# The turns of a quantized mixture of experts: down products ahead of the gate products, token copies behind rounding, more buffers

## The chip, the cores and the metric

The kernel runs on one core of a Trainium2 chip. The metric is the device time of one launch in microseconds, from the runs of the kernel; the profile comes from one further execution.

The engines go by their short names: PE is TensorE, which multiplies matrices; PEld is its loading of the stationary operand; DVE is VectorE; ACT is ScalarE; POOL is GpSimd; SP is SyncE, which only issues transfers. Each has its own list of instructions, and semaphores order them against each other.

## The reference, cut to what matters

The whole program is a decoder of two layers with six parts, over 2048 tokens (16 blocks of 128) of 256 numbers. The change touches the first part alone, a mixture of experts with weights of three values and activations of 8 bits:

```python
def activation_quant(x):
    scale = 127.0 / jnp.clip(jnp.max(jnp.abs(x), axis=-1, keepdims=True), 1e-05)
    return jnp.clip(jnp.round(x * scale), -128, 127) / scale
def weight_quant(w):
    scale = 1.0 / jnp.clip(jnp.mean(jnp.abs(w)), 1e-05)
    return jnp.clip(jnp.round(w * scale), -1, 1) / scale
def bitlinear(x, w):
    xn = rmsnorm(x, BIT_EPS)
    return activation_quant(xn) @ weight_quant(w).T      # in value
def bit_mlp(x, gate_proj_w, down_proj_w):
    gy = bitlinear(x, gate_proj_w)
    gate, y = jnp.split(gy, 2, axis=-1)
    return bitlinear(jax.nn.silu(gate) * y, down_proj_w)

shared_out = bit_mlp(x_flat, shared_gate_w, shared_down_w)
router_probs = softmax((rmsnorm(x_flat) * gate_norm_w) @ gate_w.T)
# two experts of eight per token, at most 320 tokens per expert, in the order of the tokens
for e in range(E):
    keep = sel & (jnp.cumsum(sel) <= capacity)
    routed += where(keep, w_e, 0.0)[:, None] * bit_mlp(x_flat, expert_gate_w[e], expert_down_w[e])
x = layernorm(x + routed + shared_out)
```

The gate projection makes 1024 numbers per token (512 for silu, 512 to multiply), the down projection goes from 512 back to 256.

## The kernel before

The part is the function `stage0`. Its instructions are issued in the order in which Python writes them (a manual schedule), so the code's order is each engine's order.

**Tiles, groups and turns.** A tile is 128 rows of tokens. There are 36 tiles in eight groups: three groups of the shared expert with four tiles (s0, s1, s2), four groups of routed tokens with five tiles for two experts (r0 to r3; the fifth tile is half one expert, half the other), and the last shared group s3. The main loop (L648) runs over turns: turn n works on tile n with its gate products, and on earlier tiles with the later steps.

For a tile the steps are these. `gated` (L481) multiplies the transposed tokens `xqT` with the expert's quantized weights, into the PSUM tiles ps_g and ps_y. `silu` (L492) is an ACTIVATE out of ps_g into "m_sg"; `hidden` (L497, the row L500) multiplies it on DVE with ps_y into "m_h"; `squares` (L502) sums the squares on ACT; `largest` (L506) takes the largest on DVE. When a group is through, POOL makes the reciprocal root (`K.rsqrt`) and `factors` (L510) the steps of the quantization. Then, six or seven turns after its gate products (`second`, L642), a tile is `rounded` (L517; on ACT for tiles 0 to 7, on DVE after that), `turn`ed (L524: four transposes on PE into ps_t), copied back one turn later by `turned` (L530, ACT, the row L532), multiplied by `down` (L534, PE into ps_o), and one turn after that `done` (L541) adds it to x, or scales it and stores it to `y_dram` for the routed tokens.

**Order within a turn, before.** In program order: the total of an expert's weights (`first_jobs`), the token transposes with their copies (`prepare` and `tokens`, L449), `rounded`, `done`, `squares`, `silu(n + 1)`, `hidden(n)`, `turn`, `turned`, `gated(n + 2)`, `down`, `largest`, the turn's jobs, `factors`. Read per engine this is:

- PE: total, token transposes (8 of them), turn, gate products, down, jobs;
- ACT: copy of the tokens (L455), rounded, done for odd routed tiles, squares, silu, turned, jobs;
- DVE: the factor of the tokens (L474), rounded, done, hidden, largest, jobs.

**Jobs.** Lists say which work beside the tiles goes into which turn. `made_in(e, n)` spreads the quantization of expert e's weights over turns n to n + 6: the sums of absolute values (`sum_down`, `sum_gate`), the `total` over partitions on PE, `means`, then `up` (ACT adds a large constant so that numbers are rounded, L232), `low` (DVE takes the constant off again and cuts at 1, L235) and `high` (DVE cuts at -1, L238). Experts begin in turns 0, 3, 5, 8, 10, 13, 15 and 18. Other jobs are the router (`logits`, `turn_logits`, and six pieces of `routes`, in turns 1 to 6), the quantization of the second half of the tokens (`quantized`), and `fetch`, which gathers a group's token rows from DRAM into "xe" by indirect transfers that POOL issues (L432), at the turn 6 for r0.

**Buffers.** The PSUM tags ps_g, ps_y, ps_t and ps_o have two buffers each. The tag "m_sg" has three, and it is used by `silu`, by `measured` and `quantized` (the quantization of the tokens, L250 and L269) and by `turn_logits`. The transposed tokens "xqT" have two.

Of the kernel before, what the change touches and what calls it, by code (L numbers as in the profile page):

```python
# [8 lines left out]
F32 = mybir.dt.float32  # L9
F16 = mybir.dt.float16  # L10
BF16 = mybir.dt.bfloat16
# [8 lines left out]
P = 128  # L20
NB = 16
D = 256
# [96 lines left out]
def stage0(K, ahead, late, late_dram):  # L119
# [6 lines left out]
    with ExitStack() as ctx:  # L126
# [70 lines left out]
        def weights(e):  # L197
            wf = raw[e].rearrange("p k n -> p (k n)")
            parts_of = (slice(0, 2 * 4 * D), slice(2 * 4 * D, 3 * 4 * D))
            n, bufs = ("", (5, 8)) if e < NE else ("_s", (1, 1))  # L200
            q = [K.new(wp, [P, k, 4 * D], BF16, t + n, bufs=m) for t, k, m in zip(("q", "q_d"), (2, 1), bufs)]
            qf = [t.rearrange("p k n -> p (k n)") for t in q]
            acc = K.new(small, [P, 2], F32, "w_acc")
            mean, s = (K.new(small, [P, 2], F32, t) for t in ("w_mean", "w_s"))
            back = K.new(small, [P, 2], F32, "w_back", bufs=10)
            made[e] = (q[0], q[1][:, 0, :].rearrange("p (k n) -> p k n", n=D), back)

            def sum_down():
                if e < 3:
                    nc.scalar.activation(qf[1], wf[:, parts_of[1]], AF.Abs, accum_out=acc[:, 1:2])  # L210
                else:
                    nc.vector.tensor_reduce(acc[:, 1:2], wf[:, parts_of[1]], AX.X, ALU.add, apply_absolute_value=True)

            def sum_gate():
                to = qf[0]
                if 3 <= e < NE:
                    to = K.new(work, [P, NB, P], BF16, "at_place", bufs=1).rearrange("p b n -> p (b n)")
                nc.scalar.activation(to, wf[:, parts_of[0]], AF.Abs, accum_out=acc[:, 0:1])

            def total():  # L220
                held[e] = K.new(ps, [P, 2], F32, "ps_o")
                nc.tensor.matmul(held[e], K.ones, acc, start=True, stop=True)

            def means():
                nc.vector.tensor_tensor(mean, held[e], parts, ALU.mult)
                nc.vector.tensor_scalar(mean, mean, 1e-5, None, ALU.max)
                nc.vector.reciprocal(s, mean)
                nc.vector.tensor_scalar(back, mean, 1.0 / 127.0, None, ALU.mult)

            def up(i):  # L230
                at = wf[:, parts_of[i]]
                nc.scalar.activation(at, at, AF.Identity, scale=s[:, i:i + 1], bias=magic)  # L232

            def low(i):
                nc.vector.tensor_scalar(qf[i], wf[:, parts_of[i]], MAGIC, 1.0, ALU.subtract, ALU.min)  # L235

            def high(i):
                nc.vector.tensor_scalar(qf[i], qf[i], -1.0, None, ALU.max)  # L238

            return SimpleNamespace(  # L240
                sum_down=sum_down, sum_gate=sum_gate, total=total, means=means, up=up, low=low, high=high,
            )
# [4 lines left out]
        )  # L247

        def measured(b):
            junk = K.new(work, [P, FF], F32, "m_sg", bufs=3)[:, :D]  # L250
            nc.scalar.activation(junk, x[b], AF.Square, accum_out=ss[:, b:b + 1])
            nc.vector.tensor_reduce(am[:, b:b + 1], x[b], AX.X, ALU.max, apply_absolute_value=True)

# [12 lines left out]
            nc.vector.tensor_copy(xq[:, four(g), D // 2:D // 2 + 1].bitcast(F32), ag.unsqueeze(2))  # L266

        def quantized(b):
            t = K.new(work, [P, FF], F32, "m_sg", bufs=3)[:, :D]  # L269
            nc.vector.tensor_scalar(t, x[b], rs_bit[:, b:b + 1], sc[:, b:b + 1], ALU.mult, ALU.mult)  # L270
            nc.vector.tensor_scalar(xq[:, b, :D // 2].bitcast(BF16), t, MAGIC, MAGIC, ALU.add, ALU.subtract)

# [17 lines left out]
                )  # L290

        def turn_logits():
            lgT = K.new(work, [P, FF], F32, "m_sg", bufs=3)
            nc.scalar.copy(lgT, held["lgT"])
            pt = K.new(ps, [P, 4, P], F32, "ps_t")
            for j in range(4):
                nc.tensor.transpose(pt[:, j, :], lgT[:, j * P:(j + 1) * P], K.ident)
            held["lg"] = pt.rearrange("p j (g e) -> p g j e", e=32)[:, :, :, :NE]
# [148 lines left out]
                g.backs.append(t)  # L447

        def tokens(g, t0):  # L449
            m = min(4, g.n - t0)  # L450
            pt = K.new(ps, [P, 8, P], BF16, "ps_t")
            for t in range(m):
                for k in range(KD):
                    nc.tensor.transpose(pt[:, 2 * t + k, :], g.rows[t0 + t][:, k * P:(k + 1) * P], K.identb)
            nc.scalar.copy(g.xqT[:, 2 * t0:2 * (t0 + m), :], pt[:, :2 * m, :])  # L455

        def prepare(g):

            if g.shared:
                g.use = [[(every, made[NE])]] * 4  # L460
                rows = [xq[:, 4 * g.i + t, :D // 2].bitcast(BF16) for t in range(4)]
                factor = a[:, four(g.i)]
                backs = [made[NE][2][:, i:i + 1].to_broadcast([P, 4]) for i in range(2)]
            else:
                w0, w1 = made[2 * g.i], made[2 * g.i + 1]
                g.use = [[(every, w0)]] * 2 + [[(every, w1)]] * 2 + [[(slice(0, 64), w0), (slice(64, P), w1)]]
                rows = [xe[g.i][:, t, :D // 2].bitcast(BF16) for t in range(5)]
                factor = xe[g.i][:, :, D // 2:D // 2 + 1].bitcast(F32).rearrange("p t c -> p (t c)")
                backs = g.backs
            g.bd = backs[1]  # L470
            g.xqT, g.rows = K.new(work, [P, 10, P], BF16, "xqT"), rows
            tokens(g, 0)
            g.s1 = K.new(small, [P, 5], F32, "m_s1")[:, :g.n]
            nc.vector.tensor_tensor(g.s1, factor, backs[0], ALU.mult)  # L474
            g.ss, g.am, g.rs, g.a2, g.s2, g.s3 = (
                K.new(small, [P, 5], F32, t)[:, :g.n] for t in ("m_ss", "m_am", "m_rs", "m_a2", "m_s2", "m_s3")
            )

        pg, py, sg, pt, hT, po = {}, {}, {}, {}, {}, {}

# [10 lines left out]

        def silu(n):  # L492
            g, t = tiles[n]
            sg[n] = K.new(work, [P, FF], F32, "m_sg", bufs=3)
            nc.scalar.activation(sg[n], pg[n], AF.Silu, scale=g.s1[:, t:t + 1])

        def hidden(n):  # L497
# [73 lines left out]
        w.means()  # L571
        w.up(0)
        prepare(groups[0])
        steps(1)
        for b in range(4, 8):
            quantized(b)
# [10 lines left out]
        w.low(1)  # L587
        load(2)
        w.high(1)
        for g in range(3):  # L590
            logits(g)


        jobs, first_jobs = {n: [] for n in range(N)}, {}
# [1 line left out]
        def job(n, f, *args):  # L596
            jobs[n].append((f, args))
# [21 lines left out]
            job(n + 6, call("high", 1))  # L619

        ws = {}
        job(0, logits, 3)
        job(0, turn_logits)
        for g in (2, 3):
            job(2 * g - 4, steps, g)
            for b in range(4):
                job(2 * g - 4 + b // 2, quantized, 4 * g + b)
        job(3, lambda: nc.sync.dma_start(xq_dram.rearrange("(b p) c -> p b c", p=P), xq))
        route = routes()
        for n in range(1, 7):  # L630
            job(n, next, route, None)
        for e, n in enumerate((0, 3, 5, 8, 10, 13, 15, 18)):
            made_in(e, n)
        job(11, ahead)
        job(6, fetch, 0, range(5))
        for g in groups[3:7]:
            job(g.start - 5, backs_of, g)
            if g.i:
# [6 lines left out]

        for n in range(max(second) + 3):  # L648
            r = second.get(n)
            if n in first_jobs:  # L650
                first_jobs[n]()
            if n + 2 in starts:
                prepare(starts[n + 2])
            if n + 1 in starts and starts[n + 1].n > 4:
                tokens(starts[n + 1], 4)
            if r is not None:
                rounded(r)
            if n - 2 in second:
                done(second[n - 2])
            if 0 < n <= N:  # L660
                squares(n - 1)
            if n - 1 in ends:
                g = ends[n - 1]
                K.rsqrt(small, g.rs, g.ss, 1.0 / FF, 1e-8, "m_rt")
            if n + 1 < N:
                silu(n + 1)
            if n < N:
                hidden(n)
            if r is not None:
                turn(r)  # L670
            if n - 1 in second:
                turned(second[n - 1])
            if n + 2 < N:
                gated(n + 2)
            if n - 1 in second:
                down(second[n - 1])
            if n < N:
                largest(n)
            for f, args in jobs.get(n, ()):
                f(*args)  # L680
            if n - 2 in ends:
                factors(ends[n - 2])


    def after_experts(work, small):
# [1573 lines left out]
```

## Time and profile before

| | us |
|---|---|
| runs of the kernel | 1493.09, 1498.34, 1503.92 (median 1498.34) |
| the profiled execution, its own time | 1500.89 |
| its span, first to last instruction | 1499.2 |
| mean granted TensorE clock in it | 0.933 |
| PE busy | 1285.9 |
| DVE busy | 817.3 |
| ACT busy | 662.9 |
| POOL busy | 441.3 |
| first gate product of tile 0 starts | 22.5 |
| last down product of the stage starts | 211.8 |

The span is cut into groups of equal instructions by line, engine and operation. "Busy" is the time in which an engine executes; waiting, branching and issuing transfers don't count. A wait is put down to what released it. The granted clock is the share of TensorE's full clock. Five of the six parts of the program, from about 212 us on, are not touched by the change.

### The profile page before, as it was taken

The numbers are of one execution on the slowest core, as the hardware profiler recorded it, in microseconds if no ns is written. First come the engines' busy times: TensorE is split into PE (matmuls) and PEld (weight loads), VectorE is DVE, ScalarE is ACT, GpSimd is POOL, SyncE is SP. The second block draws the span as 40 slices with busy tenths as digits, with TensorE's granted clock in tenths as the row PEclk, the third lists the DMA queues.
The fourth block names the chain that finished last, engine by engine and source line by source line (L and its number), as shares of the span: only waits on it lengthen the run. The fifth ranks groups of instructions, "written<-read, shape, count | busy, mean of one in ns | idle before, by whom it ended". The sixth has DMA issues, their size and how long they took to land.

```text
span 1499.2 us, 18888 instructions
## 1 busy us (share of the span) xinstructions
PE 1285.9 (86%) x6771; PEld 866.3 (58%) x6771; DVE 817.3 (55%) x1707; ACT 662.9 (44%) x1722; POOL 441.3 (29%) x531
## 2 busy tenths in 40 slices
PE   3366677889857999889999999999889999999995
PEld 1133344566633666566557777777677566665554
DVE  6868777989966677658444444446433411211114
ACT  5497674778933544332216554555543111111110
POOL 3223237667843645430232212122210200000003
PEclk9567898989988999998989999999999999999997
DMA  8164124111000000001000000001003123312102
GB/s 281 30 229 134 45 63 81 16 37 57 29 1 0 1 1 1 0 1 57 1 1 1 2 0 1 1 17 55 14 1 127 56 99 99 98 68 94 39 12 70
DMA packets 50541, 71.98 MB, mean 48 GB/s; under 512 B 10224, under 2 KB 39888, under 8 KB 50192
## 3 DMA queue, kind: packets, MB, share of 16 engines
q1 hardware_dynamic: 48272, 65.24, 13.1%
q0 software_dynamic: 2176, 5.55, 1.8%
q8 instruction: 53, 0.87, 0.2%
q14 instruction: 40, 0.33, 0.1%
HBM read 60.77 MB, written 5.80 MB: 44 GB/s over the span
## 4 chain that ended last, share of the span: by engine, by line
PE 66%; DVE 18%; ACT 5%; POOL 5%; issue 3%; DMA 1%; SPq 0%; ACTq 0%; DVEq 0%; POOLq 0%
PE ps_m L1648 7%; PE ps_y L2093 7%; PE ps_m L2082 7%; PE ps_g L2082 6%; PE ps_m L1668 4%; PE ps_m L1779 4%; PE ps_m L1236 2%; PE ps_s L1737 2%; PE ps_t L1770 2%; PE ps_y L1362 2%; PE ps_t L1759 2%; PE ps_seg L1304 2%; PE ps_y L1342 2%; DVE s L867 1%; PE ps_m L1330 1%
## 5 line engine op out<-in xcount | busy, mean ns | idle before, releaser
L2087 DVE TENSOR_TENSOR h<-h,ps_m 128x512 f32<-128x512 f32 x60 | 41.3, 689 | 226.5 <-PE ps_m L2082 226.5
L82 POOL TENSOR_SCALAR ln_t<-ln_mv 128x1 f32<-128x1 f32 (+1 forms) x84 | 16.2, 193 | 454.0 <-DVE ln_mv L90 309.5
L1750 ACT ACTIVATE s<-s,m 128x128 f32<-128x128 f32 x256 | 99.5, 391 | 53.7 <-DVE m L1744 53.7
L2086 ACT ACTIVATE h<-ps_g 128x512 f32<-128x512 f32 x60 | 35.8, 597 | 171.6 <-PE ps_g L2082 171.6
L2082 PE MATMUL ps_g<-xin,w 128*128 128x512 f32 x224 | 106.3, 592 | 0.0
L1754 POOL TENSOR_TENSOR s<-s,t 128x1024 f32<-128x1024 f32 x32 | 60.9, 1902 | 152.6 <-DVE t L1753 152.6
L2082 PE MATMUL ps_m<-xin,w 128*128 128x512 f32 x224 | 105.3, 592 | 0.0
L2093 PE MATMUL ps_y<-w,h 128*128 128x256 f32 x448 | 97.8, 379 | 0.0
L2093 PEld LDWEIGHTS ps_y<-w,h 128*128 128x128 f32 x448 | 85.1, 190 | 14.6 <-issue 3.3
L879 ACT ACTIVATE s<-s,m 128x128 f32<-128x128 f32 x256 | 83.2, 394 | 15.7 <-DVE m L874 15.7
L2082 PEld LDWEIGHTS ps_m<-xin,w 128*128 128x128 f32 x224 | 42.5, 190 | 51.4 <-issue 50.2
L2082 PEld LDWEIGHTS ps_g<-xin,w 128*128 128x128 f32 x224 | 42.0, 190 | 46.4 <-issue 45.0
L1740 DVE TENSOR_TENSOR s<-ps_s,hide 128x1024 f32<-128x1024 f32 x32 | 39.2, 1224 | 52.1 <-PE ps_s L1737 52.0
L1648 PE MATMUL ps_m<-ctxT,l1x_W_k 128*128 128x256 f32 x256 | 63.9, 398 | 1.6 <-DVE qT L1653 1.0
L1762 DVE COPY s<-ps_t 128x512 f32<-128x512 f32 x32 | 22.1, 690 | 76.4 <-PE ps_t L1759 76.4
L1648 PE MATMUL ps_m<-xT,half 128*128 128x256 f32 x256 | 61.2, 393 | 2.6 <-DVE qT L1653 1.9
L1668 PE MATMUL ps_m<-l1x_W_v,ctxT 128*128 128x512 f32 x128 | 62.1, 614 | 0.0
L1779 PE MATMUL ps_m<-half,oT 128*128 128x256 f32 x256 | 59.3, 385 | 0.0
L528 PE MATMUL ps_t<-ident,m_h 128*128 128x128 f32 x144 | 29.0, 336 | 34.5 <-ACT m_h L520 14.1
L1242 DVE SCALAR_TENSOR_TENSOR acc<-ps_m,l1a_conv_w,acc 128x508 f32<-128x508 f32 (+2 forms) x72 | 52.6, 735 | 10.6 <-ACT acc L1238 10.5
L2094 ACT COPY y<-ps_y 128x256 f32<-128x256 f32 x30 | 11.2, 372 | 104.7 <-PE ps_y L2093 66.2
L1648 PEld LDWEIGHTS ps_m<-xT,half 128*128 128x128 f32 x256 | 48.5, 194 | 11.2 <-DVE qT L1653 2.3
(497 smaller groups left out, 3116.9 us busy)
## 6 DMA issues: line engine op xcount, KB each, us to landing
w<-in_w_gate_dram SPq DMA_DIRECT2D x9, 1024.0 KB
w<-in_l1f_gateT_dram SPq DMA_DIRECT2D x14, 512.0 KB
w<-in_l1f_upT_dram SPq DMA_DIRECT2D x14, 512.0 KB
w<-in_l1f_downT_dram SPq DMA_DIRECT2D x14, 512.0 KB
w<-in_w_down_dram SPq DMA_DIRECT2D x9, 512.0 KB
ring<-y SPq DMA_DIRECT2D x128, 32.0 KB
y_dram<-y SPq DMA_DIRECT2D x20, 128.0 KB
x<-in_x_dram SPq DMA_DIRECT2D x16, 128.0 KB
```

The source lines that it names most:

```text
L879: nc.scalar.activation(at, at, AF.Exp, bias=m[h][:, i:i + 1])
L1242: nc.vector.scalar_tensor_tensor(accv[:, :, j:], pcv[:, :, :P - j], w.conv[:, c, TAPS - 1 - j:TAPS - j], accv[:, :, j:], ALU.mult, ALU.add,)
L1648: nc.tensor.matmul(pq[:, j, :], wt[k][:, at], src[:, k, :], start=(k == 0), stop=(k == KD - 1))
L1668: nc.tensor.matmul(pv, self.ctxT[:, k, b * P:(b + 1) * P], self.w.v[:, k, 512 * j:512 * j + 512], start=(k == 0), stop=(k == KD - 1),)
L1740: nc.vector.tensor_tensor(half(b, j), pss.rearrange("p r c k -> p (r c) k"), hide.unsqueeze(1).to_broadcast([P, 8, P]), ALU.add,)
L1750: nc.scalar.activation(at, at, AF.Exp, bias=m[j][:, i:i + 1], accum_out=t[j][:, i:i + 1])
L1754: nc.gpsimd.tensor_tensor(half(b, j), half(b, j), t[j].unsqueeze(2).to_broadcast([P, 8, P]), ALU.mult)
L1779: nc.tensor.matmul(py[b], oT[b][:, c, :], w.o[c // 4][:, c % 4, :], start=(c == 0), stop=(c == NC - 1))
L2082: nc.tensor.matmul(ps[:, j, :], m[k][:, c * P:(c + 1) * P], self.r.xin[:, k, e, cols], start=(k == 0), stop=(k == KD - 1),)
L2086: nc.scalar.activation(h, pg, AF.Silu)
L2087: nc.vector.tensor_tensor(h, h, pu, ALU.mult)
L2093: nc.tensor.matmul(pd, rows(c), w.down[c // 4][:, c % 4, :], start=(c == 0), stop=(c == FI // P - 1))
```

## The change

It has five pieces.

1. The order within a turn becomes: total, `rounded`, `turned`, copy of the tokens, `hidden`, `silu`, `turn`, `down`, `gated`, `squares`, `done`, `largest`, jobs, `factors`, `scaled`, then `prepare` and the token transposes. Per engine: PE has total, turn, down, gate products, jobs, token transposes; ACT has rounded, turned, copy of the tokens, silu, squares, done, jobs; DVE has rounded, hidden, done, largest, jobs, factor of the tokens.
2. `tokens` returns its copy as a function, which is called in the next turn. The transposes of a group start at the end of the third turn ahead of it, instead of the head of the second.
3. For experts 0 and 1 the low step is done by ACT (constant taken off), and the cut at 1 joins the cut at -1 on DVE.
4. `measured` and `quantized` get buffers of their own ("m_q", three of half the size), and "m_sg" gets four.
5. The logits move into turns 0 and 1, `turn_logits` to turn 1, the six pieces of `routes` to turns 2 to 7, and r0's `fetch` to turn 7.

```diff
             def low(i):
-                nc.vector.tensor_scalar(qf[i], wf[:, parts_of[i]], MAGIC, 1.0, ALU.subtract, ALU.min)
+                if e < 2:
+                    nc.scalar.activation(qf[i], wf[:, parts_of[i]], AF.Identity, bias=unmagic)
+                else:
+                    nc.vector.tensor_scalar(qf[i], wf[:, parts_of[i]], MAGIC, 1.0, ALU.subtract, ALU.min)
             def high(i):
-                nc.vector.tensor_scalar(qf[i], qf[i], -1.0, None, ALU.max)
+                if e < 2:
+                    nc.vector.tensor_scalar(qf[i], qf[i], 1.0, -1.0, ALU.min, ALU.max)
+                else:
+                    nc.vector.tensor_scalar(qf[i], qf[i], -1.0, None, ALU.max)
...
-            junk = K.new(work, [P, FF], F32, "m_sg", bufs=3)[:, :D]
+            junk = K.new(work, [P, D], F32, "m_q", bufs=3)
...
-            t = K.new(work, [P, FF], F32, "m_sg", bufs=3)[:, :D]
+            t = K.new(work, [P, D], F32, "m_q", bufs=3)
...
-            nc.scalar.copy(g.xqT[:, 2 * t0:2 * (t0 + m), :], pt[:, :2 * m, :])
+            return lambda: nc.scalar.copy(g.xqT[:, 2 * t0:2 * (t0 + m), :], pt[:, :2 * m, :])
...
-            sg[n] = K.new(work, [P, FF], F32, "m_sg", bufs=3)
+            sg[n] = K.new(work, [P, FF], F32, "m_sg", bufs=4)
...
-        for g in range(3):
-            logits(g)
-        job(0, logits, 3)
-        job(0, turn_logits)
+        for g in range(4):
+            job(g // 2, logits, g)
+        job(1, turn_logits)
-        for n in range(1, 7):
+        for n in range(2, 8):
             job(n, next, route, None)
-        job(6, fetch, 0, range(5))
+        job(7, fetch, 0, range(5))
...
         for n in range(max(second) + 3):
             r = second.get(n)
             if n in first_jobs:
                 first_jobs[n]()
-            if n + 2 in starts:
-                prepare(starts[n + 2])
-            if n + 1 in starts and starts[n + 1].n > 4:
-                tokens(starts[n + 1], 4)
             if r is not None:
                 rounded(r)
-            if n - 2 in second:
-                done(second[n - 2])
+            if n - 1 in second:
+                turned(second[n - 1])
+            if turned_tokens is not None:
+                turned_tokens()
+                turned_tokens = None
+            if n < N:
+                hidden(n)
+            if n + 1 < N:
+                silu(n + 1)
+            if r is not None:
+                turn(r)
+            if n - 1 in second:
+                down(second[n - 1])
+            if n + 2 < N:
+                gated(n + 2)
             if 0 < n <= N:
                 squares(n - 1)
...
-            if n + 1 < N:
-                silu(n + 1)
-            if n < N:
-                hidden(n)
-            if r is not None:
-                turn(r)
-            if n - 1 in second:
-                turned(second[n - 1])
-            if n + 2 < N:
-                gated(n + 2)
-            if n - 1 in second:
-                down(second[n - 1])
+            if n - 2 in second:
+                done(second[n - 2])
...
+            if n + 2 in starts:
+                scaled(starts[n + 2])
+            if n + 3 in starts:
+                prepare(starts[n + 3])
+                turned_tokens = tokens(starts[n + 3], 0)
+            if n + 2 in starts and starts[n + 2].n > 4:
+                turned_tokens = tokens(starts[n + 2], 4)
```

`scaled` is the product of the tokens' factors (L474 before), taken out of `prepare`.

More of the change, by code (lines that the diff above doesn't have):

```diff
@@ L292, in turn_logits @@
         def turn_logits():
-            lgT = K.new(work, [P, FF], F32, "m_sg", bufs=3)
+            lgT = K.new(work, [P, FF], F32, "m_sg", bufs=4)
             nc.scalar.copy(lgT, held["lgT"])
@@ L470, in prepare, with scaled @@
             g.bd = backs[1]
[L471 to L476, printed above, removed]
-            )
+            g.xqT, g.rows, g.first = K.new(work, [P, 10, P], BF16, "xqT"), rows, (factor, backs[0])
+            g.s1, g.ss, g.am, g.rs, g.a2, g.s2, g.s3 = (
+                K.new(small, [P, 5], F32, t)[:, :g.n] for t in ("m_s1", "m_ss", "m_am", "m_rs", "m_a2", "m_s2", "m_s3")
+            )
+        def scaled(g):
+            nc.vector.tensor_tensor(g.s1, *g.first, ALU.mult)
         pg, py, sg, pt, hT, po = {}, {}, {}, {}, {}, {}
@@ L573, in stage0 @@
         prepare(groups[0])
+        tokens(groups[0], 0)()
+        scaled(groups[0])
         steps(1)
@@ L627, in stage0 @@
                 job(2 * g - 4 + b // 2, quantized, 4 * g + b)
+        job(1, turn_logits)
         job(3, lambda: nc.sync.dma_start(xq_dram.rearrange("(b p) c -> p b c", p=P), xq))
-        route = routes()
-        for n in range(1, 7):
-            job(n, next, route, None)
         for e, n in enumerate((0, 3, 5, 8, 10, 13, 15, 18)):
             made_in(e, n)
+        route = routes()
+        for n in range(2, 8):
+            job(n, next, route, None)
         job(11, ahead)
-        job(6, fetch, 0, range(5))
+        job(7, fetch, 0, range(5))
         for g in groups[3:7]:
@@ L651, in stage0 @@
                 first_jobs[n]()
[L652 to L655 removed]
             if r is not None:
                 rounded(r)
[L658 to L659 removed]
+            if n - 1 in second:
+                turned(second[n - 1])
+            if turned_tokens is not None:
+                turned_tokens()
+                turned_tokens = None
+            if n < N:
[8 more added lines that the diff above has]
+                gated(n + 2)
             if 0 < n <= N:
```

## The prediction

> **What bounds the kernel now.** I read the page's 40 slices first: the change touches only the first stage (the quantized experts), so I looked for that stage's end and its busy shares. The last down product of the stage starts at 211.8 us; everything behind it (86% of the span) keeps its instructions, so a gain here counts once, in full. Then I cut the stage at the starts of the products L500 of tiles 0, 7, 22 and 35 (25.6, 80.5, 155.3, 200.3 us) and asked for the busy time per stretch. Columns: stretch, length, then PE, PEld, DVE, ACT, POOL, and the granted clock.
>
> ```profile
> 25.60:80.50 54.90, 21.98 (x109) 9.88 (x108) 40.79 (x122) 28.03 (x41) 10.38 (x8) 0.59 0.31 107
> 80.50:155.30 74.80, 47.80 (x222) 27.11 (x222) 56.27 (x124) 62.18 (x96) 23.92 (x45) 0.75 0.50 164
> 155.30:200.30 45.00, 30.71 (x193) 18.31 (x194) 31.57 (x70) 31.57 (x66) 11.01 (x19) 0.88 0.14 46
> 200.30:212.40 12.10, 9.78 (x71) 6.84 (x69) 7.71 (x21) 6.62 (x12) 1.33 (x2) 0.88 0.19 66
> ```
>
> No engine is full. DVE leads in the first stretch (14.1 us idle), ACT in the second (12.6 idle), nobody in the third (13.4 idle on both). So I read the view of waits of each stretch for the engine that leads it.
>
> First stretch, DVE (and ACT behind it):
>
> ```profile
> DVE m_sg L270 <- PE ps_t L297: 4.4, 1, 4.4
> DVE m_sg L270 <- ACT m_sg L504: 3.2, 1, 3.2
> DVE whose L411 <- PE ps_o L406: 2.8, 1, 2.8
> ACT m_h L520 <- DVE m_s L514: 7.7, 1, 7.7
> PE ps_y L487 <- DVE m_h L500: 14.2, 4, 5.8
> ```
>
> Two waits, 7.6 us, are for a free "m_sg" buffer: L270 shares its three with silu, `measured` and `turn_logits`. The last two lines show ACT and PE waiting for DVE.
>
> Second stretch:
>
> ```profile
> ACT xqT L455 <- PE ps_t L454: 12.6, 6, 3.4
> DVE x L546 <- PE ps_o L539: 11.8, 5, 3.2
> PE ps_t L528 <- ACT xqT L455: 2.7, 3, 1.1
> DVE m_s L474 <- DMA xe<-xq_dram,token: 2.6, 1, 2.6
> ```
>
> The first line is all of ACT's idle time: the copy of the transposed tokens stands at the head of ACT's turn, and PE reaches the transposes only after its own previous turn and the weight total. The second is DVE's: `done` stands ahead of `hidden`, and its down product is PE's last act of the turn before.
>
> Third stretch, waits and then the chain that ended last (start, us, what):
>
> ```profile
> DVE y L552 <- PE ps_o L539: 9.9, 7, 2.3
> ACT xqT L455 <- PE ps_t L454: 8.1, 3, 3.9
> ACT y L550 <- PE ps_o L539: 5.4, 5, 1.2
> DVE m_s L474 <- DMA xe<-xq_dram,token: 2.8, 1, 2.8
> ```
>
> ```profile
> 193.22 0.69 ACT m_hT L532
> ...
> 193.96 0.62 PE ps_o L539 x4
> ...
> 194.60 0.48 DVE y L552
> 195.09 0.67 DVE m_h L500
> ...
> 195.80 0.59 PE ps_y L487 x2
> 196.39 0.45 PE ps_o L539 x4
> ...
> 196.87 0.47 ACT y L550
> ```
>
> This is a ring through four engines: turned, down, done, hidden, gate products, down, done, squares, silu, turned. It closes at 198.53, 5.3 us for two turns.
>
> **What the Trainium skill says.** "TensorE: Matmul & The Clock Gate", section on the array of 32×32 sub-arrays: PE may pull weight loads ahead, but matmuls keep their order, and ACT and DVE take instructions strictly in order. The trace agrees: squares, silu and turned all sit behind the copy that waits 12.6 us. "Perfetto Trace Analysis", section Optimization Strategy under Identifying Performance Opportunities: equal bubbles that return can mean too few buffers; the two m_sg waits are that. The first page's section "What's actually happening" has PE at half clock until it has been busy for some microseconds; here the clock is 0.59 and 0.75 in stretches where PE is 40% and 64% busy, and the four transposes L528 take 1.11 us slow and 0.66 us fast. "SBUF — State Buffer", section "SBUF: two separate sides": DVE and POOL exclude each other on a shared port pair. L235 of expert 0 took 1.75 and 1.21 us while POOL worked on L395 (68.67 to 72.96), 1.22 and 0.69 otherwise.
>
> **The change, part by part.**
>
> *m_q beside m_sg (three buffers of its own, m_sg four).* The 4.4 and 3.2 us waits go: -7.6 on DVE, which leads there.
>
> *Low steps of experts 0 and 1 on ACT.* Two ACTIVATEs per expert. No row has this form; bounds are the row L232 (2.09 and 1.24 us, two pointer operands) above and L218 and L210 (1.90 and 1.05) below. I take 2.0 and 1.1, which is also the estimate from "ScalarE: Activation LUTs", section What ACT_TABLE_LOAD costs (280 ns + 0.833 per element with a pointer bias: 1.99 and 1.13). ACT +3.1 per expert. DVE loses 1.75 + 1.21 = 3.0 for expert 0, 1.9 for expert 1; `high` gains an operand and stays one pass (0.68 + 0.42). Expert 0's falls in turn 5, where ACT waits for DVE (28.0 busy of 54.9): hidden, -3.0. Expert 1's falls in turn 8, where ACT leads: +3.1. Behind it on ACT stand turn 9's rounding, turned and silu; PE waits for them.
>
> *Logits, turn_logits and routes a turn later; fetch in turn 7.* The moved work is equal: 16 matmuls, one copy (0.59), the DVE rows of the router, exp with its table loads, five gathers on POOL and the semaphores they wait for. The last piece (`whose`, `token`, 0.6 us, and the 2.8 us wait ahead of it) leaves the stretch before tile 7: -3.4 for that stretch, most of which the next one may pay as idle DVE time, where DVE has 18 us to spare. The gathers have less slack: issue to landing was 79.9 to about 88 us, and the transposes that need them stand two to three turns later, at some 5 us each. At nothing, up to +3. On SP the xq_dram store keeps turn 3; the weight load behind expert 0's and 1's low now waits for ACT instead of DVE, earlier in time.
>
> *Copies a turn later than their transposes.* In PE's order the eight transposes only move from the head of a turn to the end of the one before; what they pass is the weight total, which waits for ACT's last job. On ACT the copy moves behind rounded and turned. Eleven copies. In the second stretch six waits cost 12.6. The one at 123.57 (2.8) is partly the gather's landing (DVE L474 waits for the same DMA) and stays; of the other 9.8 I keep 1.7, since there are only two ps_t buffers and PE's turn transposes now wait for ACT's turned (0.7) after a token turn: -8.1.
>
> *Turned and down in front of the gate products, hidden in front of done, silu in front of squares.* Nothing is added. The ring above is cut: done no longer stands before hidden, so the 11.8 us (DVE, second stretch: not the leader, no gain of its own) and the 9.9 + 5.4 us (third stretch) lose their reason. The new wait: gate products now queue behind down, which waits for turned on ACT; silu of the next turn waits for them. From turned: 0.62 down + 0.55 first gate half (fast clock), while ACT has silu 0.57 and squares 0.62 to do. Even; so no stall at full clock.
>
> **Sum.** First stretch: -7.6 - 3.0 - 3.4 = -14.0; DVE then works 37 of 41 us, and I give 4 us back for waits that the trace doesn't show yet (means for the weight total, the cumulative sum's matmul): -10. Second: -8.1 + 3.1 = -5; at best -9.5 (all 12.6 gone, +3.1), at worst +3. Third: 13 turns at 3.46 us; the work of a turn at full clock is PE 0.66 + 0.62 + 1.1 = 2.4, DVE 31.57/13 = 2.4, ACT 2.4. I take 2.9, which leaves room for r3's gathers, whose 2.8 us wait stays: 13 x 2.9 = 38, -7 (between -2 and -11). Last: the drain has the same steps, 0. Together -22 us on the profiled execution's 1500.89 us (span 1499.2), which is 2.55 above the median of the runs, 1498.34: 1478.9 by its own scale, about 1477 by the median.
>
> **The rivals.**
>
> *A. The leading engine sets the pace, and only the buffers help.* I summed each turn's work on ACT and on DVE and took the larger: 172 us over turns 0 to 34, where the trace has 174.7 (25.6 to 200.3). By that count turns are already paced by their fullest engine, and reordering inside a turn gains little. For it: this agreement, and the second stretch, where ACT is 83% busy. Against: the third stretch, 45.0 against 40.4. It would give -9 us: 1489.
>
> *B. Full decoupling.* All engines run a turn ahead; each stretch comes to its leader's work plus 3 us: 41, 68, 36 instead of 54.9, 74.8, 45.0: about -30 to -36, 1464. Against: gathers and the long jobs (2 us ACTIVATEs) come in lumps.
>
> *C. Slower: the gate products behind down.* PE stays near half clock after 80 us. Then a turn on PE is 1.1 + 0.85 + 1.7, tokens and totals 0.4, and 0.5 waiting for turned with nothing else allowed past: 4.6 us. Over 28 turns (7 to 34) that is 129 us against 119.8: +9, and with only 3 us won in the first stretch +6: 1504. It decides once the granted clock is below about 0.6 in the second and third stretch; it was 0.75 and 0.88. For it: before, gate products never had to wait for the same turn's turned.
>
> *D. The change does nothing*, because a buffer ties the copy and the turn transposes together (two ps_t): within 3 us. I count it with A.
>
> **How the numbers follow.** Main case 0.5 (own range 1467 to 1488), A and D 0.24, B 0.19, C 0.07. Measured differences under about 1% (1483.4 to 1513.3) can't be told from no change. Faster by over 1%: 0.43 of the main case, B, and a little of A, 0.65. Slower by over 1%: 0.03, the tail of C. The rest, 0.32, is within. The range runs from B's 1461 to 1494, which leaves out C, part of D and B's best.
>
> **What would show it.** In the trace after: tile 7's product near 70 us instead of 80.5, no DVE wait for m_q; copies of tokens without more than 1 us of ACT idle before them, save r1 and r3; DVE not waiting for the down product; the third stretch under 40 us; the last down product near 190 us, and the rest unmoved at 1287 us. I am wrong if silu waits for gate products turn after turn (C), if ACT is over 90% busy in the second stretch at the same length (A), or if the gathers of r0 come late.

## The result and the profile after

The changed kernel takes 1481.08 us (median of 5 runs, 1476.46 to 1485.84), the kernel before 1498.34. The ratio is 0.9885, with an interval of 0.9847 to 0.9924; a second series gave 0.9891 (0.9871 to 0.9912). It is faster by 1.1%; 1477 us was predicted. But one of the three stretches of the stage became longer where the prediction had it shorter, and that stretch is what the experiments are about.

Stretches are read as before, at the starts of the product that makes the hidden values (now L507) of tiles 0, 7, 22 and 35, and at the end of the last down product (now L546). Busy time by stretch of the kernel after, columns as before (length; PE, PEld, DVE, ACT, POOL; granted clock):

```profile
23.90:68.60 44.70, 23.01 (x108) 10.68 (x107) 38.89 (x118) 32.22 (x45) 9.22 (x6) 0.71 0.42 143
68.60:146.20 77.60, 46.54 (x225) 27.68 (x225) 53.88 (x125) 62.63 (x92) 29.23 (x47) 0.69 0.48 158
146.20:184.30 38.10, 27.75 (x193) 16.81 (x190) 30.27 (x68) 31.28 (x66) 11.60 (x19) 0.96 0.16 51
184.30:195.80 11.50, 8.90 (x72) 6.55 (x72) 7.97 (x22) 7.50 (x15) 1.41 (x2) 1.00 0.23 82
```

First stretch 54.9 to 44.7, second 74.8 to 77.6, third 45.0 to 38.1, drain 12.1 to 11.5. In the second stretch ACT, its fullest engine, is busy for 62.6 us as for 62.2 before, and PE and DVE for less than before, so its 2.8 us are new idle time of these engines.

First stretch, the waits that answer to those of before (engine, line, releaser: us in total, times, longest):

```profile
PE ps_y L494 <- DVE m_h L507: 6.7, 3, 4.7
ACT m_h L527 <- DVE m_s L521: 6.1, 1, 6.1
DVE whose L415 <- PE ps_o L412: 1.9, 1, 1.9
```

The two waits of L270 for an "m_sg" buffer are gone. Second stretch:

```profile
POOL m_rt L82 <- ACT m_sg L511: 30.9, 2, 16.7
ACT xqT L462 <- PE ps_t L461: 12.0, 5, 7.1
DVE w_mean L225 <- PE ps_o L222: 11.3, 3, 6.5
...
DVE m_a L518 <- POOL m_rs L83: 9.0, 1, 9.0
PE ps_t L461 <- DMA xe<-xq_dram,token: 8.5, 5, 3.6
...
POOL m_b L452 <- DMA xe<-xq_dram,token: 4.6, 1, 4.6
```

DVE hardly waits for the down product here any more (0.5 us in place of 11.8), as forecast. But ACT's copy of the tokens still waits 12.0 us (12.6 before), and what stands behind that wait is new: PE waits 8.5 us at the token transposes for gathered rows, and DVE waits 9.0 us once for a root on POOL.

The timelines of DVE and POOL show that one wait (start, duration, engine, line; the idle time before it and its releaser in brackets):

```profile
76.66 0.43 DVE L242 TENSOR_SCALAR q_d<-q_d 128x1024 bf16<-128x1024 bf16 x1
86.09 0.16 DVE L518 TENSOR_TENSOR m_a<-m_am,m_rs 128x4 f32<-128x4 f32 x1 [9.01 <-POOL m_rs L83]
```

```profile
83.73 0.18 POOL L452 COPY m_b<-w_back 64x1 f32<-64x1 f32 x1 [4.65 <-DMA xe<-xq_dram,token]
...
84.74 0.19 POOL L82 TENSOR_SCALAR m_rt<-m_ss 128x4 f32<-128x4 f32 x1
85.02 1.04 POOL L83 TENSOR_TENSOR m_rs<-m_rt,mhalf 128x4 f32<-128x4 f32 x1
```

POOL had issued r0's five gathers (71.9 to 78.7 us), then stood in the copy of r0's weight scales L452 until they had landed, with the root of group s1 behind it. The copy reads only scales, no gathered rows, and yet the profile puts the end of its wait to the gathers; why it waits for them is not shown.

The timelines of POOL and PE around r1's gathers:

```profile
100.26 0.20 POOL L82 TENSOR_SCALAR m_rt<-m_ss 128x4 f32<-128x4 f32 x1 [14.20 <-ACT m_sg L511]
...
104.70 1.07 POOL L438 DMA_INDIRECT xe<-xq_dram,token  x1 [0.28 <-POOL m_b L452]
...
110.27 2.52 POOL L438 DMA_INDIRECT xe<-xq_dram,token  x1 [0.30 <-issue]
```

```profile
110.91 0.77 PE L461 MATMUL ps_t<-identb,xe 128*128 128x128 bf16 x4 [2.93 <-issue]
113.74 0.40 PE L461 MATMUL ps_t<-identb,xe 128*128 128x128 bf16 x2 [2.06 <-DMA xe<-xq_dram,token]
117.76 0.40 PE L461 MATMUL ps_t<-identb,xe 128*128 128x128 bf16 x2 [3.62 <-DMA xe<-xq_dram,token]
117.94 0.53 PE L222 MATMUL ps_o<-w_acc,ones 128*128 128x2 f32 x2
```

The gathers queue on POOL behind a root (L82) that waited 14.2 us for ACT's squares of tile 11. PE meets the rows before they are there and stands in order; the weight total L222 behind it is what DVE's 6.5 us wait for.

Third stretch, waits and the chain of work that ended last (start, us, what):

```profile
ACT xqT L462 <- issue: 5.4, 1, 5.4
...
PE ps_o L546 <- ACT m_hT L539: 4.1, 5, 2.0
DVE m_s L484 <- DMA xe<-xq_dram,token: 4.0, 1, 4.0
PE ps_t L461 <- DMA xe<-xq_dram,token: 3.8, 4, 1.1
```

```profile
174.00 1.02 ACT xqT L462
...
175.60 0.61 ACT m_sg L511 x2
176.21 0.58 ACT m_hT L539
176.79 0.58 ACT m_sg L502
177.37 0.57 ACT m_sg L511 x2
```

In this piece the chain is ACT's own work but for a pair of gate products at 175.07; `done` is not in it, and the ring through four engines is cut. Further on (179.8 to 184.4) it runs through POOL's root and DVE's factors. The wait of down for turned (4.1 us in five) is the new wait that the prediction named, small as it said. What is left is again gathers, those of r3; the 5.4 us at ACT's copy, for which the view names no releaser, stand before r3's copy too.

The profiled execution spans 1474.7 us, 24.5 less than before: 16.6 in the stage and 7.9 in the rest, whose instructions did not change. By the medians of the runs the gain is 17.3 us, near the stage's 16.6; the last section comes back to the rest.

### The profile page after: what moved, and what is told of

Read it like the earlier page. It is cut to its first block, busy times and chain, and to the rows that moved or that the text cites. A ratio compares the mean times of both kernels' runs of the same rounds, so it can differ in the third digit from the quotient of the medians.

```text
span 1474.7 us, 18916 instructions
## 1 busy us (share of the span) xinstructions
PE 1273.7 (86%) x6771; PEld 862.8 (59%) x6771; DVE 809.4 (55%) x1703; ACT 667.3 (45%) x1726; POOL 445.0 (30%) x531
## 4 chain that ended last, share of the span: by engine, by line
PE 64%; DVE 19%; POOL 6%; ACT 4%; issue 4%; DMA 2%; SPq 0%; DVEq 0%; POOLq 0%; ACTq 0%
PE ps_y L2108 7%; PE ps_m L2097 7%; PE ps_g L2097 7%; PE ps_m L1663 6%; PE ps_m L1794 4%; PE ps_m L1683 3%; PE ps_m L1251 3%; PE ps_s L1752 2%; PE ps_t L1785 2%; PE ps_y L1377 2%; PE ps_t L1774 2%; PE ps_y L1357 2%; PE ps_seg L1319 1%; DVE s L882 1%; PE ps_m L1345 1%
## 5 line engine op out<-in xcount | busy, mean ns | idle before, releaser
L82 POOL TENSOR_SCALAR ln_t<-ln_mv 128x1 f32<-128x1 f32 (+1 forms) x84 | 16.1, 192 | 451.6 <-DVE ln_mv L90 309.5
L2109 ACT COPY y<-ps_y 128x256 f32<-128x256 f32 x30 | 11.2, 372 | 104.7 <-PE ps_y L2108 64.6
L1663 PEld LDWEIGHTS ps_m<-ctxT,l1x_W_k 128*128 128x128 f32 x256 | 47.8, 195 | 9.3 <-DVE qT L1668 1.4
```

The lines of the kernel that those rows point to most:

```text
L1663: nc.tensor.matmul(pq[:, j, :], wt[k][:, at], src[:, k, :], start=(k == 0), stop=(k == KD - 1))
```

## The experiments

Theory P: time was lost because POOL stands in r0's scale copies until the gathers land. Theory G: the gathers of r1 to r3 come too late for transposes that now stand earlier. Rival Q: ACT is the bound of the second stretch, and waits elsewhere cost nothing. Each kernel was timed against the kernel before on the same chip. Stretches are of one profiled execution each; two executions of the changed kernel differ by up to 1.1 us in a stretch.

| kernel | first | second | third | whole, ratio to before (interval) |
|---|---|---|---|---|
| before | 54.9 | 74.8 | 45.0 | 1 |
| changed | 44.7 | 77.6 | 38.1 | 0.9885 (0.9847 to 0.9924) |
| changed, second series | 45.8 | 77.4 | 38.8 | 0.9891 (0.9871 to 0.9912) |
| scale copies of r0 first | 45.9 | 71.5 | 38.0 | 0.9880 (0.9855 to 0.9904) |
| gathers a turn earlier | 45.6 | 74.3 | 32.3 | 0.9832 (0.9806 to 0.9858) |
| both | 45.5 | 67.8 | 31.6 | 0.9805 (0.9781 to 0.9828) |
| low steps on DVE | 47.8 | 75.3 | 39.0 | 0.9922 (0.9905 to 0.9939) |
| both, copies at once | 45.3 | 67.8 | 34.8 | 0.9827 (0.9809 to 0.9845) |
| both, low of expert 1 on DVE | 45.7 | 68.5 | 32.5 | 0.9815 (0.9795 to 0.9834) |
| gathers ahead of the root | 45.9 | 68.7 | 33.5 | 0.9813 (0.9798 to 0.9829) |
| both, routes as before | 46.8 | 70.3 | 31.4 | 0.9812 (0.9796 to 0.9828) |
| before + buffers | 49.3 | 73.9 | 44.1 | 0.9954 (0.9936 to 0.9971) |
| before + order | 57.0 | 79.2 | 40.4 | 1.0013 (0.9999 to 1.0026) |
| before + order + gathers early | 57.5 | 70.5 | 35.1 | 0.9933 (0.9918 to 0.9949) |

**Scale copies of r0 first** (from the changed kernel).

```
-            job(g.start - 5, backs_of, g)
+            job(g.start - (5 if g.i else 6), backs_of, g)
```

> The changed kernel, but POOL copies the weight scales of r0 (L449 to L452) in turn 6, ahead of the five gathers instead of behind them; nothing else moves. Theory P (in the second stretch, tile 7 to tile 22, the time was lost because POOL stands in L452 until r0's gathers have landed, and the root of group s1 behind it holds DVE's factors L518 for 9.0 us): that wait falls under 3 us, the second stretch goes from 77.6 us to 71 to 74, the whole by 4 to 7 us to about 1475. Theory Q (ACT is the bound of this stretch, and idle time of DVE is bought there): the wait goes, but the stretch stays above 76 and the whole within 2 us of 1481. Theory G (only the late landing counts): the wait passes to PE at r0's transposes L461, and the stretch stays.

Its waits in the second stretch:

```profile
PE ps_t L461 <- DMA xe<-xq_dram,token: 9.0, 5, 4.6
...
DVE m_a L518 <- POOL m_rs L83: 3.1, 1, 3.1
```

DVE's wait for the root falls from 9.0 to 3.1 us, the stretch to 71.5. The copies, now ahead of the gathers, wait for nothing. P holds, by one edit on POOL that changes nobody's work (ACT is busy for 63.0 us, 62.6 before the edit), and Q falls. The whole does not show it (0.9880): 6.1 us in the stretch are within what the rest of the program varied by.

**Gathers of r1 to r3 a turn earlier** (from the changed kernel).

```
-            job(g.start - 5, backs_of, g)
+            job(g.start - (6 if g.i else 5), backs_of, g)
-                job(g.start - 5, fetch, g.i, range(0, 2))   # and -4, -3
+                job(g.start - 6, fetch, g.i, range(0, 2))   # and -5, -4
```

> The changed kernel, but the scale copies and gathers of r1, r2 and r3 are issued one turn earlier (six, five and four turns ahead of their group instead of five, four and three). r0's stay. Theory G (PE stands in order at the token transposes L461 until a gather lands; 8.6 us at r1, 2.8 at r2, 3.9 at r3): PE's wait for the gathers falls from 12.3 us to under 5, the second stretch from 77.6 to 70 to 74, the third from 38.1 to 35 to 37, the whole by 5 to 9 us to about 1474. Theory Q (ACT is the bound): the waits go and the two stretches shorten by under 2 us together. Theory C (the gathers are slow because weight loads share the DMA engines): issued earlier they land no earlier against those loads, and the waits stay over 9 us.

PE's wait for gathers falls from 12.3 to 2.4 us in the two stretches. Second stretch 74.3, a little less of a gain than expected, third 32.3, more than expected, the whole at 0.9832: G holds, theory C of the weight loads falls, and the third stretch, which I had priced as settled, had 5.8 us in it.

**Both edits.**

> The changed kernel with both edits: the scale copies of r0 ahead of its gathers, and the copies and gathers of r1, r2 and r3 one turn earlier. If P and G hold and name different waits, the gains add: second stretch 65 to 70 us (my forecast for the change itself was 69.8), whole 1467 to 1472. If ACT is the bound (Q), the second stretch is not under 75 and the whole about 1479 to 1481.

```profile
69.30:137.10 67.80, 43.04 (x227) 24.44 (x225) 54.30 (x124) 64.42 (x94) 28.11 (x56) 0.76 0.56 181
137.10:168.70 31.60, 25.78 (x190) 15.98 (x190) 30.20 (x68) 29.13 (x64) 9.56 (x10) 1.00 0.19 61
```

The gains add, 9.8 us in the second stretch. ACT is now busy for 64.4 of 67.8 us, which looks like rival Q; that ACT bounds the stretch is not shown, and the experiment on expert 1's low step below speaks against it. The median was 1464.82 us (the kernel before on that chip 1494.71). It is the shortest median of the study, and its interval lies wholly below the changed kernel's; it can't be told from the variants of it below.

**A turn, or a place in the queue?** The scale copies and all five gathers of a group are issued in the turn of the changed kernel's first two gathers, but ahead of POOL's root; r0's scale copies come first.

```
-                job(g.start - 5, fetch, g.i, range(0, 2))
-                job(g.start - 4, fetch, g.i, range(2, 4))
-                job(g.start - 3, fetch, g.i, range(4, 5))
...
+            if n in ahead_of_root:                 # n = start - 5 of r1, r2, r3
+                backs_of(ahead_of_root[n])
+                fetch(ahead_of_root[n].i, range(5))
             if n - 1 in ends:
                 g = ends[n - 1]
                 K.rsqrt(small, g.rs, g.ss, 1.0 / FF, 1e-8, "m_rt")
```

> The changed kernel with r0's scale copies ahead of its gathers, and the scale copies and all five gathers of r1, r2 and r3 in the same turn as in the changed kernel (five ahead of their group), but issued on POOL ahead of the root of the group that ends there instead of behind it. Theory R (gathers came late because POOL stood in that root, L82, for ACT's squares, which the change moves to the end of the turn): the gain of moving them a whole turn is had without it: second stretch 66 to 70, third 31 to 34, PE's wait at L461 for gathers under 3 us, whole 1464 to 1468. Theory T (the gathers simply need a turn more, whatever stands ahead): second stretch stays at 71 to 73 and third at 37 to 38.

POOL's timeline, at the place of r1's gathers:

```profile
87.77 1.06 POOL L438 DMA_INDIRECT xe<-xq_dram,token  x1 [0.28 <-POOL m_b L452]
...
92.93 0.94 POOL L438 DMA_INDIRECT xe<-xq_dram,token  x1 [0.30 <-issue]
97.42 0.20 POOL L82 TENSOR_SCALAR m_rt<-m_ss 128x4 f32<-128x4 f32 x1 [3.54 <-ACT m_sg L511]
```

They are issued from 87.8 instead of 104.7 us, nobody waits for a gather any more in the two stretches, and these are 68.7 and 33.5: theory R. The edit does not hold turn and queue fully apart, since three of the five gathers, which stood one and two turns later in the changed kernel, move up in program order as well. But in the changed kernel's trace all five go out in one run behind the root (104.7 to 112.8 us, 0.3 us between them), so it was the root that held them. And a turn of lead works the same way: in the kernel with both edits r1's first two gathers go out at 87.6 and 88.9 us, ahead of the root at 97.4, and the other three behind it. The gathers stood in line behind a root that had nothing to do with them.

**The order inside a turn alone** (from the kernel before; turned, hidden and silu, turn, down, gate products, squares, root, done).

> The kernel before with the order inside a turn alone (turned, hidden and silu, turn, down, gate products, squares, root, done); token copies, buffers, routes and low steps stay as before. My term: third stretch 45.0 to 38 (the change's own 38.1), first within 2 us of 54.9, DVE's and ACT's waits for the down product (9.9 and 5.4 us in the third stretch) under 2 us. Rival C (gate products behind down cost PE more than the ring gives back): third stretch 45 or more. For the second stretch (74.8): under 73 if the cut ring helps there too, over 76 if the root behind the later squares holds the gathers on POOL, as the trace of the changed kernel suggests.

Its waits in the second stretch:

```profile
DVE m_s L474 <- DMA xe<-xq_dram,token: 13.2, 2, 8.4
DVE m_a L511 <- POOL m_rs L83: 4.2, 1, 4.2
```

Third stretch 40.4: 4.6 of its 7 us come from the order alone, the waits of DVE and ACT for the down product are gone there, and rival C falls for this stretch. The second becomes 4.4 us longer, the first 2.1, so that the whole gains nothing. Over the three stretches DVE waits 19.2 us and PE 9.4 for gathers, where before it was 5.4 and 1.1.

**The same with the gathers early.**

> The kernel before with the order inside a turn alone (first 57.0, second 79.2, third 40.4), plus r0's scale copies ahead of its gathers and the copies and gathers of r1 to r3 one turn earlier. If the order's loss in the second stretch is the gathers' (DVE waited 19.2 us and PE 9.4 for them), the second stretch falls to 70 to 74, below the 74.8 of the kernel before, and the third to 35 to 38; the whole 1482 to 1487. If the order itself costs there (gate products behind down at the lower clock), the second stretch stays at 77 or more.

Second stretch 79.2 to 70.5, third 40.4 to 35.1: the order's loss was the gathers', and rival C falls for the second stretch too. Order and early gathers together are worth 4.3 and 9.9 us against the kernel before. What early gathers are worth there without the order was not run, so these gains are not the order's alone. The first stretch stays at 57.5; what costs 2 us there was not pursued.

**Copies of tokens at once** (from the kernel with both edits).

```
-                turned_tokens = tokens(starts[n + 3], 0)
+                tokens(starts[n + 3], 0)()
...
-                turned_tokens = tokens(starts[n + 2], 4)
+                tokens(starts[n + 2], 4)()
```

> The kernel with scale copies ahead and gathers one turn earlier (67.8 us in the second stretch, 31.6 in the third), but each copy of tokens L462 is issued at once behind its transposes instead of a turn later. My term for the copies was 8.1 us in the second stretch: then it comes to 74 to 77, with ACT waiting 8 us or more for L461. Rival: with the new order inside the turn PE reaches the transposes early, the copy waits under 3 us, and the stretch stays at 67 to 70.

ACT's waits in the second stretch:

```profile
ACT xqT L462 <- PE ps_t L461: 3.4, 3, 1.9
```

The rival holds: the second stretch does not move. In the third the later copies are worth 3.2 us. My 8.1 us were not there.

**Low steps on DVE**: both (in the changed kernel), and expert 1's alone (in the kernel with both edits).

> The changed kernel, but the low steps of experts 0 and 1 are back on DVE (and high has one operand less, as in the kernel before). My prediction's terms: first stretch +3.0 us (44.7 to 47.7), second stretch -3.1 (77.6 to 74.5), whole unchanged within 1 us. Rival: both stretches wait for something else (first for the router's chain, second for gathers), and neither moves by over 1.5 us. Second rival: DVE is the busier engine in both, and the whole becomes 3 to 5 us longer.

> The kernel with scale copies ahead and gathers one turn earlier, and besides expert 1's low step back on DVE (expert 0's stays on ACT). From the run with both low steps on DVE (first stretch +3.0, second -2.3): second stretch 67.8 to 65 to 66, the others unmoved, whole 1462 to 1463 against 1464.8. Rival: the 2.3 us came from where the gathers fell, and the second stretch stays at 67 to 69.

First stretch +2.3 us against the mean of five kernels with the low step on ACT (45.5): near the 3.0. In the second stretch 2.2 us came back in the changed kernel, but none with the gathers out of the way (68.5 against 67.8): the rival of the second expectation. ACT's added 3.1 us of expert 1 did not cost what I charged. The second stretch with expert 1's step on DVE:

```profile
70.92:139.38 68.46, 43.39 (x224) 25.30 (x225) 55.51 (x126) 60.00 (x92) 29.00 (x56) 0.74 0.54 179
```

ACT is busy for 4.4 us less than with both edits (60.0 for 64.4), and the stretch is no shorter, so ACT's work alone does not bound it.

**Routes as before** (from the kernel with both edits: `next(route)` in turns 1 to 6, r0's gathers in 6, its scale copies in 5).

> The kernel with scale copies ahead and gathers one turn earlier (first stretch 45.5, second 67.8), with the router's pieces in turns 1 to 6 and r0's gathers in turn 6 as in the kernel before (the copies of r0's scales in turn 5). My term for moving them a turn later was -3.4 us in the first stretch: then the first stretch comes to 48 to 49.5 and the second to 65 to 68, since the same work is then done ahead of it. Rival: the pieces fit in DVE's idle time either way, the first stretch stays within 1.5 us of 45.5 and the second too.

First stretch +1.3, little more than two executions of one kernel differ by, second +2.5. Moving the router's pieces later is worth some 1.3 us in the first stretch, not 3.4. The second did not fall as expected. In part the line between the stretches cuts elsewhere: ACT is busy for 29.1 and 66.9 us in the two, 32.2 and 64.4 with both edits. The two together are 3.8 us longer; why was not pursued, and the whole (0.9812) cannot be told from 0.9805.

**Buffers alone** (from the kernel before).

> The kernel before with the buffers alone: m_q with three buffers for L253 and L274, m_sg with four. My term for it: the DVE waits of L270 for m_sg (4.4 and 3.2 us) go, first stretch 54.9 to about 47.3, second and third within 1.5 us of 74.8 and 45.0, whole 1498 to about 1491. Rival: another wait takes the place (the quantizing steps reach POOL's and the router's rows no earlier), first stretch over 52.

DVE's waits in the first stretch:

```profile
DVE whose L411 <- PE ps_o L406: 2.7, 1, 2.7
DVE pr L307 <- PE ps_t L297: 2.2, 1, 2.2
```

First stretch -5.6: the two waits are gone, and 2.0 of the 7.6 us came back, with L307's wait for the router's transposes as the new one. The whole is at 0.9954.

**The changed kernel again.**

> The changed kernel once more, so that it is timed against the kernel before on the same chip as the next three, and its stretches are seen a second time. Stretches within 1.5 us of 44.8, 77.6 and 38.1; the ratio 0.985 to 0.992. Whether the rest of the program (1278.9 us in the first profile, 1286.8 in the kernel before, with the same instructions) is shorter because of the change: if so it stays near 1279; if it is the granted clock of that one execution, it may be anything from 1276 to 1287.

The stretches repeat; the rest takes 1279.9 us, near the first profile's 1278.9. By itself that would fit a shorter rest because of the change; the other profiles, in the last section, speak against it.

## Why the prediction was right, and which term was not

*First stretch, -10 predicted, -10.2 (second series -9.1) measured: right.* Its parts measured alone were smaller: buffers -5.6 for -7.6, low step -2.3 for -3.0, routes -1.3 for -3.4, and the order +2.1 where I had nothing. Their sum is -7.1: together they gave 2 to 3 us more than one by one, and which of them needs which stays open. That the sum came out is in part luck: the terms were too large, and the 4 us that I gave back for waits not yet seen covered it. The ACTIVATE of the low step took 2.00 and 1.14 us, as estimated.

*Second stretch, -5 predicted, +2.8 measured: wrong.* The step that failed is the cost of the gathers, "at nothing, up to +3". Freeing them is worth 9.8 us here and 6.5 in the third stretch. I had looked at r0's five gathers and their distance in turns, and missed how POOL holds them. r1's stood behind a root before the change too, and that root waited longer; these are two of POOL's waits in the second stretch of the kernel before:

```profile
POOL m_rt L82 <- ACT m_sg L504: 34.2, 2, 18.4
...
POOL m_b L446 <- DMA xe<-xq_dram,token: 1.3, 1, 1.3
```

But PE then came to r1's rows 9.7 us after their first issue (112.3 to 122.0), and comes after 6.2 us now, and waits. The order inside a turn is enough for this: in the kernel with the order alone, where the token transposes stand where they stood, it is 6.1 us (117.9 to 124.0). In ACT's turn the squares, on which the root waits, now stand behind turned and silu, 1.1 us behind the start of turned (98.32 to 99.45); I wrote of this part "nothing is added". What the earlier place of the transposes adds was not measured apart. For r0, POOL stands in the scale copy until the gathers have landed: that wait was 1.3 us before and is 4.6 now, with a root behind it.

The other term, -8.1 for the copies, was mis-sized too: ACT's 12.6 us of idle time were real, but taking them away is not worth as much. Against the kernel before with order and early gathers (70.5), where ACT still waits 9.3 us for the copies, everything else in the kernel with both edits, where it waits 1.1, brings 2.7 us. Why is not shown; rival A, who held that reordering gains little where the fullest engine already sets the pace, was nearer in this stretch. The +3.1 of expert 1's low step was no cost either. That the total came out near (-22 forecast, -17 by the medians) is owed to the other stretches, which hit.

*Third stretch, -7 predicted, -6.9 measured: right*, for the larger part by the mechanism named: the ring is cut, DVE and ACT do not wait for down, the clock is 0.96, and the order alone gives 4.6. But the later copies, for which I put nothing here, were worth 3.2 with the gathers early, and the room that I left for r3's gathers was too small: freeing the gathers is worth 6.5, and -13.4 (31.6) was possible, beyond my best bound of -11.

*Drain, 0 predicted, -0.6.* Of the marks: tile 7's product stands at 68.6 (near 70), the last down ends at 195.8 (near 190), the rest takes 1278.9 (1287), L462 waits more than 1 us also at r2, and "if the gathers of r0 come late" was the sign that came. The kernel with both edits comes to rival B's sum over the three stretches, 144.9 us for 145, though not stretch by stretch (45.5, 67.8 and 31.6 for 41, 68 and 36). That its median, 1464.82, also meets B's 1464 is luck, since the kernel before ran 3.6 us faster on that chip. Most of what full decoupling promised was there to be had, and the gathers kept it away.

## What to carry to other kernels

When work is moved within a turn, list for each engine what it issues for others behind the moved instruction: here squares on ACT held a root on POOL, the root held gathers that share only the queue with it, and those held PE, three steps from the edit. Put transfers ahead of any instruction on the issuing engine that waits for a slow producer; here that gave 68.7 us, and a whole turn of lead, which put the first of them ahead of it too, 67.8. The idle time of a leading engine is not what its removal gains (here a wait that fell from 9.3 to 1.1 us, together with other changes, brought 2.7), so test such a term by an edit of its own before it is priced.

## What the runs showed of the hardware

**POOL is slow beside DVE's low steps.** On POOL's timeline of the changed kernel a copy of two elements per partition takes 1.22 us, and on DVE's a low step lies at just that time:

```profile
101.51 1.22 POOL L449 COPY m_b<-w_back 128x2 f32<-128x2 f32 x1
102.67 0.66 POOL L450 COPY m_b<-w_back 128x2 f32<-128x2 f32 x1
103.27 0.18 POOL L451 COPY m_b<-w_back 64x1 f32<-64x1 f32 x1
...
103.75 0.18 POOL L449 COPY m_b<-w_back 128x2 f32<-128x2 f32 x1
```

```profile
101.47 1.22 DVE L238 TENSOR_SCALAR q<-w 128x2048 bf16<-128x2048 f32 x1
102.60 0.69 DVE L238 TENSOR_SCALAR q_d<-w 128x1024 bf16<-128x1024 f32 x1
```

The same copy beside no such step takes 0.18 us, and the next group's copies, at 131.25 and 132.55 us, again take 1.25 and 0.55 beside low steps. The issue of a gather is longer as well: 2.52 us at 110.27, beside L238 from 110.16 to 111.98, where the other four of the group take 0.94 to 1.37. The Trainium skill has this in "DMA: Bandwidth & Descriptors", section SWDGE vs HWDGE vs iDMA: POOL writes the descriptors of its DMAs into SBUF, and DVE can lock it out of SBUF while it runs in a mode that uses two ports. The trace agrees in the times, though it does not show DVE's mode; by them the lock-out cost that gather about 1.5 us, an estimate from 2.52 and about 1.0.

**The clock of unchanged code varies.** Ten microseconds, from 90 us behind the stage's end, before and after:

```profile
302.40:312.40 10.00, 9.28 (x33) 7.03 (x33) 7.14 (x14) 4.37 (x12) 5.25 (x8) 0.50 0.00 0
```

```profile
285.80:295.80 10.00, 9.78 (x89) 7.53 (x89) 8.52 (x17) 8.38 (x25) 6.49 (x9) 0.89 0.00 0
```

PE is busy nearly throughout, and the granted clock is 0.50 in one and 0.89 in the other. Both windows begin at about the same place of the program, but in these 10 us PE makes 33 products in one and 89 in the other. The same eight products in both:

```profile
306.83 2.08 PE L860 MATMUL ps_s<-kT,qT 32*128 32x256 f32 x8
```

```profile
288.40 1.13 PE L875 MATMUL ps_s<-kT,qT 32*128 32x256 f32 x8
```

Of the fourteen profiles six have a clock of 0.50 to 0.59 in this window, and eight 0.83 to 0.89. The rest of the program took 1281.6 to 1286.8 us in the six and 1275.5 to 1283.6 in the eight, with no relation to the edits that I could see (1279.0 with the buffers alone, 1286.4 with the scale copies first), so the 7.9 us of the first profile are not counted for the change. What sets the clock there was not tried.
